# A sparse-attention kernel: the second tile's key products placed behind the first tile's scaling and statistics, and half of the feed-forward weights loaded by another queue

## The chip, the core and the metric

The kernel runs on one core of a Trainium2 chip. A core has TensorE (PE, matrix products), VectorE (DVE), ScalarE (ACT), GpSimd (POOL) and SyncE (SP), which run side by side and wait for each other through semaphores; each takes its own instructions strictly in the order in which they were written into its queue. Sixteen DMA engines move data between the large memory (HBM) and the on-chip memory. The metric is the time of one execution on the device, in microseconds (us); the time before is 1765.6 us, the median of three runs (1764.82 to 1766.44).

## The reference

One layer of attention over a sparse graph, with a feed-forward part. There are 4096 nodes of 512 features, 8 heads of 64. `adj` is a 4096 x 4096 mask with about 17 neighbours per node.

```python
hs, ht = layer_norm(x), layer_norm(h_target)
q = (ht @ Wq + bq) / 8;  k = hs @ Wk + bk;  v = hs @ Wv + bv      # split in 8 heads
logits = where(adj != 0, q . k, -1e30)                            # per head
ctx = softmax(logits) @ v
ht = ht + ctx @ Wo + bo
ht = layer_norm(ht)
out = layer_norm(x + ht + gelu(ht @ W1) @ W2)                     # W1: 512 x 2048, W2: 2048 x 512
```

## The kernel before

The kernel never forms the 4096 x 4096 logits. It works in two stages that overlap a little.

In the first stage (to about 270 us of the trace) PE projects all of `x` to keys and values and ScalarE writes them to a table `kvd` in HBM, one row of 1024 numbers (key and value) per node. Meanwhile the adjacency rows are turned into lists of neighbours, and the nodes are sorted by their number of neighbours. Nodes are then taken in 32 tiles of 128, `TILES`; a tile has a cap, the largest number of neighbours its nodes may have. The first tiles have caps 11, 13, 14, and so on. The tiles are taken in groups (`GROUPS`): the first three tiles alone, the rest mostly in pairs.

The second stage, `attention()`, takes each tile's neighbours in steps of `S = 3`. For each step:

- POOL issues one gather per neighbour (`issue`, L987): 128 rows of `kvd`, 512 KB, into a slot of a ring of 17 slots of on-chip memory. It does so ahead of use, and waits when the slot isn't free.
- VectorE multiplies the gathered keys by the tile's queries (L1277, the *key product*) and sums per head (L1283).
- ScalarE takes the exponential (L1289, L1304 for a tile's first step, and L1255).
- The values are multiplied by these weights: two of three by VectorE (L1224, the *value product*), the third by ScalarE in eight scalings, one per head (L1258).
- PE adds up the values of all neighbours, transposed, in the accumulator `cps` (L1237).

When a tile's last step is done, `finish` divides by the sum of the weights. VectorE takes the reciprocal (L1123); ScalarE spreads it over the features (L1126); PE transposes it (L1132); ScalarE copies it (L1134); VectorE multiplies the accumulator by it (L1137, the *scaling*). PE then multiplies by `wo` (L1149), ScalarE copies the result to `h` (L1155), VectorE takes mean and variance of it (L697, L698) and adds a small constant (L680, in `shifted`); these are the *statistics*. POOL raises to the power -1/2 (L687), VectorE forms the shift factor (L692), ScalarE normalizes (L1169), PE transposes (L1178), ScalarE copies (L1182).

With that, the feed-forward part of the group (`feed`) can start: PE multiplies by `W1` (L1396), ScalarE applies the gelu (L1399, with a load of its function table whenever the function changes), PE multiplies by `W2` (L1405). `end` adds, normalizes and scatters the rows to the output. `front` makes the queries of a later tile: a gather of `h_target`, a normalization by ScalarE (L1026), transposes (L1030, L1033), a product with `wq` on PE (L1040) and a bias on VectorE (L1045).

`W1` and `W2` are loaded in four quarters of 1 MB each (`load_quarter`, L586 and L587). The first two quarters are loaded in the first stage by SP. The last two fit only when the first stage's buffers are free; ScalarE issues them (`weights`), behind the last of the value scalings traced by then (`newest`). They follow each other within the trace at 304 to 306 us.

The order of instructions: the streams (`attention`, `feed`, `weights`, lists for the second half of the nodes) are generators, and `_weave` takes them in turn by the costs that they yield. What comes out is a preferred order. A scheduler then places each instruction on its engine by that order and by a model of when its inputs are ready, so that an instruction may be placed ahead of others traced earlier. `tc.issue_after(ins)`, and the helper `behind([...])` which takes the last of a list, keep it from that: the instruction is placed behind `ins` on the same engine. That is an order only, not a wait for a semaphore.

In the kernel before, `closing` holds the first tile's reciprocal and its scaling. The second tile's next key product is placed behind the reciprocal (`closing[:1]`), the sum that follows behind the scaling, and `closing` is then empty.

Of the kernel before, what the change touches and what calls it, by code (L numbers as in the profile page):

```python
# [19 lines left out]
EPS = 1e-5  # L20
# [423 lines left out]
def adj_resnorm_kernel(  # L444
# [33 lines left out]
    nc = tc.nc  # L478
# [24 lines left out]
    S = 3  # L503
# [29 lines left out]
    with tc.tile_pool(name="keep", bufs=1) as keep:  # L533
# [17 lines left out]
        with ExitStack() as late:  # L551
# [28 lines left out]

            w1, w2 = [], []

            def load_quarter(pool, q, engine=nc.sync):
                w1.append(pool.tile([P, KC, D], F32, name=f"w1_{q}"))
                w2.append(pool.tile([P, KC, D], F32, name=f"w2_{q}"))
                engine.dma_start(w1[q], W1[:, q * D:(q + 1) * D].rearrange("(c p) n -> p c n", p=P))  # L586
                engine.dma_start(w2[q], W2[q * D:(q + 1) * D, :].rearrange("(c p) n -> p c n", p=P))  # L587

# [84 lines left out]
            def rstd_of(pool, mv, n, name):  # L673

                rs = power(pool, mv, n, name)
                return rs, negmean(pool, mv, rs, n, name)

            def shifted(pool, mv, n, name):
                ve = pool.tile([P, n], F32, name=name + "_ve")
                nc.vector.tensor_scalar_add(ve, mv[:, :, 1], EPS)  # L680
                return ve

            def power(pool, mv, n, name, ve=None):
                if ve is None:
                    ve = shifted(pool, mv, n, name)
                rs = pool.tile([P, n], F32, name=name + "_rs")
                nc.gpsimd.tensor_tensor(rs, ve, mhalf[:, :n], ALU.pow)  # L687
                return rs

            def negmean(pool, mv, rs, n, name):  # L690
                nm = pool.tile([P, n], F32, name=name + "_nm")
                nc.vector.scalar_tensor_tensor(nm, mv[:, :, 0], -1.0, rs, op0=ALU.mult, op1=ALU.mult)  # L692
                return nm

            def stats(pool, src, mv, name):
                st = pool.tile([P, 6], F32, name=name + "_st")
                nc.vector.bn_stats(st, src)  # L697
                nc.vector.bn_aggr(mv, st)  # L698
# [19 lines left out]
            def behind(ins):  # L718
                return tc.issue_after(ins[-1]) if ins else nullcontext()
# [261 lines left out]


            recs, tqs, h2Ts, done, ready, latest, newest = {}, {}, {}, set(), [], [], []
            issues, logits, closing = [], [], []

            def gather(dst, table, idx):
                issues[:] = [nc.gpsimd.indirect_dma_start(  # L987
# [121 lines left out]
            def finish(i, p, cps, group, hs, mv):  # L1109


                rec, tq, cap = recs[i], tqs.pop(i), TILES[i][1]
                slow = 0 if i < QUICK else 1
                first = i == 0

                nc.vector.scalar_tensor_tensor(p[:, :cap, :], rec[:, E0:E0 + cap].unsqueeze(2)
                                               .to_broadcast([P, cap, H]), 0.0, p[:, :cap, :],
                                               op0=ALU.is_gt, op1=ALU.mult)
                nc.vector.tensor_reduce(sums[:, i, :], p[:, :cap, :].rearrange("p j h -> p h j"),
                                        AX.X, ALU.add)  # L1120
                ri = sp.tile([P, H], F32, name="ri")
                nc.vector.tensor_scalar_max(ri, sums[:, i, :], SUM_LO)
                recip = nc.vector.reciprocal(ri, ri)  # L1123
                rx = sp.tile([P, KC, P], F32, name="rb", bufs=1)
                rxf = rx.rearrange("p c t -> p (c t)")
                nc.scalar.copy(rxf.rearrange("p (h d) -> p h d", h=H),  # L1126
                               ri.unsqueeze(2).to_broadcast([P, H, HD]))
                for _ in range(0 if first else 1 + slow):
                    yield
                prx = ps.tile([P, KC, P], F32, name="t", bufs=2)  # L1130
                for c in range(KC):
                    nc.tensor.transpose(prx[:, c, :], rxf[:, c * P:(c + 1) * P], ident)  # L1132
                ct = sp.tile([P, KC, P], F32, name="rb", bufs=1)
                nc.scalar.copy(ct, prx)  # L1134
                for _ in range(0 if first else 1 + slow):
                    yield
                scaled = nc.vector.tensor_mul(ct, cps, ct)  # L1137
                if first:
                    closing[:] = [recip.ins, scaled.ins]
                for _ in range(0 if first else 1 + 3 * slow):  # L1140
                    yield
                pa = ps.tile([P, D], F32, name="t", bufs=2)

                for c in range(KC):
                    nc.tensor.matmul(pa[:, c * P:(c + 1) * P], tq[:, D + c * P:D + (c + 1) * P],
                                     ident, is_transpose=True, start=c == 0, stop=False,
                                     skip_group_check=True)
                for c in range(KC):
                    nc.tensor.matmul(pa, ct[:, c, :], wo[:, c, :], start=False,  # L1149
                                     stop=c == KC - 1, skip_group_check=True)  # L1150
                turned.add(i)
                if i > 2:
                    yield
                h = sp.tile([P, D], F32, name="h")
                nc.scalar.copy(h, pa)  # L1155
                yield
                stats(sp, h, mv[:, len(hs), :], "n2")
                hs.append(h)
                if len(hs) < len(group):
                    return  # L1160
                nh = len(hs)
                ve = shifted(sp, mv[:, :nh, :], nh, "n2")
                if i > 2:
                    yield
                rs = power(sp, mv[:, :nh, :], nh, "n2", ve)
                yield
                nm = negmean(sp, mv[:, :nh, :], rs, nh, "n2")
                for j, h in enumerate(hs):
                    nc.scalar.activation(h, h, AF.Identity, bias=nm[:, j:j + 1], scale=rs[:, j:j + 1])  # L1169
                for _ in range(0 if first else 1 + slow):  # L1170
                    yield
                w = len(hs) * P
                h2T = sp.tile([P, KC, 2 * P], F32, name="h2T")
                for k2 in range(KC // 2):
                    pt = ps.tile([P, 2, 2 * P], F32, name="t", bufs=2)
                    for k in range(2):
                        for j, h in enumerate(hs):
                            nc.tensor.transpose(pt[:, k, j * P:(j + 1) * P],  # L1178
                                                h[:, (k2 * 2 + k) * P:(k2 * 2 + k + 1) * P], ident)
                    for k in range(2):  # L1180
                        kc = k2 * 2 + k
                        nc.scalar.activation(h2T[:, kc, :w], pt[:, k, :w], AF.Identity,  # L1182
                                             bias=b2c[:, kc:kc + 1], scale=s2c[:, kc:kc + 1])
                h2Ts[GROUPS.index(group)] = h2T
# [22 lines left out]
            def attention():  # L1207
# [55 lines left out]
                for group in GROUPS:  # L1263
                    hs = []
                    mv = sp.tile([P, 2, 2], F32, name="mv2")
# [3 lines left out]
                    for i in group:  # L1269
                        cps = ps.tile([P, KC, P], F32, name="cps", bufs=2)  # L1270
                        while k < len(SG) and SG[k][0] == i:
                            _, j0, n = SG[k]
                            while i not in tqs:
                                step(fronts, i)
                            kv, tq = kvs.pop(k), tqs[i]
                            with behind(closing[:1]):
                                nc.vector.tensor_tensor(kv[:, :n, :D], kv[:, :n, :D],  # L1277
                                                        tq[:, :D].unsqueeze(1)
                                                        .to_broadcast([P, n, D]), ALU.mult)
                            lg = sp.tile([P, S, H], F32, name="lg")  # L1280
                            latest[:] = [lg[:, 0, 0:1]]
                            with behind(closing):
                                logits[:] = [nc.vector.tensor_reduce(  # L1283
                                    lg[:, :n, :],
                                    kv[:, :n, :D].rearrange("p j (h d) -> p j h d", h=H),
                                    AX.X, ALU.add).ins]
                            closing.clear()
                            if j0 > 0:
                                nc.scalar.activation(p[:, j0:j0 + n, :], lg[:, :n, :], AF.Exp)  # L1289
                            add_up()  # L1290
# [16 lines left out]
                            last = j0 + n == TILES[i][1]  # L1307
# [196 lines left out]
            def fill():  # L1504
# [4 lines left out]
                for cost in _take(ed, FILL * steps):  # L1509
                    yield cost  # L1510

            att = attention()
            _weave((projections(), 0), (prepare(), 0), (fill(), 0))
            src.close()
# [5 lines left out]
            def weights():  # L1520


                for q, pool in enumerate(pools):
                    yield 26.0 if q == 0 else 6.0
                    with tc.issue_after(newest[-1]):
                        load_quarter(pool, q + 2, nc.scalar)

            def other_lists():
                for _ in range(2):
# [44 lines left out]
```

## Time and profile before

| | |
|---|---|
| median of three runs | 1765.6 us |
| the profiled execution | 1769.85 us |
| its span, first to last instruction | 1768.1 us |
| PE busy | 1655.2 us, 94% |
| VectorE busy | 1424.7 us, 81% |
| ScalarE busy | 1234.9 us, 70% |
| GpSimd busy | 1029.6 us, 58% |
| bytes moved by DMA | 461 MB, 260 GB/s over the span |
| mean granted PE clock | 0.975 |

The profiled execution is one execution; its time is that of the span and a little around it. Busy time is the time in which an engine executes something; PE's matmuls overlap, so a busy PE need not be at its peak. PEld is PE's loading of the stationary operand. A wait "X <- Y" means that the instruction X stood idle until Y released it. "issue" is idle time in which the profile shows no wait for another engine. In lists of instructions a form such as `kv<-kv,tq` names what is written and what is read; L1277 is line 1277 of the kernel.

### The profile page before, as it was taken

To read this page: it belongs to the slowest core of one execution; us is meant where nothing else is said; L and a number is where in the kernel's file an instruction comes from. 1 tells how busy PE (TensorE), PEld (TensorE's weight loads), DVE (VectorE), ACT (ScalarE), POOL (GpSimd) and SP (SyncE) were. 2 spreads that over 40 slices of the span, in tenths; PEclk is the share of its full clock that TensorE was granted. 3 is DMA by queue.
4 is the path that set the end of the run, shared out by engine and by line. 5 is a ranking of instruction groups with operands and counts; after the bars stand their busy time and mean duration, and the time that the engine had idled before them with its cause. 6 is when DMAs were issued, how large, how long until landed. Compare 5 with 4: busy or idle time off the path is not lost. (4 is left out here: it accounts for less than half of the span.)

```text
span 1768.1 us, 22715 instructions
## 1 busy us (share of the span) xinstructions
PE 1655.2 (94%) x6978; PEld 1078.4 (61%) x6978; DVE 1424.7 (81%) x2452; ACT 1234.9 (70%) x3133; POOL 1029.6 (58%) x824
## 2 busy tenths in 40 slices
PE   7999996599899999898899999999999999999997
PEld 3444443477676667665566667666666666666665
DVE  6887787489898989897888999989898788999300
ACT  5776663479787988675667878787778687878311
POOL 1000155557565676677787788777787868675101
PEclk9999998799999999998999999999999999999999
DMA  9999978958887897677787888886877767775000
GB/s 352 372 399 361 358 242 288 354 174 285 308 273 275 328 332 266 224 256 239 245 304 270 297 286 313 278 280 222 263 261 249 250 226 260 228 257 201 22 2 26
DMA packets 141610, 461.00 MB, mean 261 GB/s; under 512 B 18036, under 2 KB 23048, under 8 KB 141480
## 3 DMA queue, kind: packets, MB, share of 16 engines
q0 software_dynamic: 96272, 342.33, 57.1%
q1 hardware_dynamic: 37392, 94.06, 15.0%
q10 hardware_dynamic: 7816, 23.08, 3.3%
q8 instruction: 57, 0.93, 0.2%
q14 instruction: 73, 0.60, 0.1%
HBM read 430.61 MB, written 28.79 MB: 260 GB/s over the span
## 5 line engine op out<-in xcount | busy, mean ns | idle before, releaser
L987 POOL DMA_INDIRECT kv<-kvd,rec x603 | 791.8, 1313 | 322.2 <-issue 133.1
L1396 PE MATMUL pf<-h2T,w 128*128 128x256 f32 (+1 forms) x2304 | 467.9, 357 | 4.4 <-ACT h2T L1182 4.0
L1405 PE MATMUL po<-w,gt 128*128 128x512 f32 x1024 | 465.2, 597 | 5.0 <-ACT gt L1399 5.0
L1396 PEld LDWEIGHTS pf<-h2T,w 128*128 128x128 f32 x2304 | 393.8, 191 | 65.8 <-issue 19.5
L1277 DVE TENSOR_TENSOR kv<-kv,tq 128x1536 f32<-128x1536 f32 (+2 forms) x211 | 351.6, 1678 | 65.9 <-DMA kv<-kvd,rec 50.3
L1258 ACT ACTIVATE kv<-kv,pa 128x64 f32<-128x64 f32 x1520 | 391.8, 340 | 3.8
L1283 DVE TENSOR_REDUCE lg<-kv 128x24 f32<-128x1536 f32 (+2 forms) x211 | 350.5, 1669 | 0.2
L1405 PEld LDWEIGHTS po<-w,gt 128*128 128x128 f32 x1024 | 189.3, 192 | 203.2 <-issue 194.7
L1237 PE MATMUL cps<-ident,kv 128*128 128x128 f32 x1828 | 243.2, 279 | 53.9 <-DVE kv L1224 32.5
L1237 PEld LDWEIGHTS cps<-ident,kv 128*128 128x128 f32 x1828 | 217.7, 144 | 121.6 <-issue 48.5
L1224 DVE TENSOR_TENSOR kv<-kv,p 128x1024 f32<-128x1024 f32 (+1 forms) x211 | 251.5, 1196 | 19.7 <-ACT p L1289 19.2
L687 POOL TENSOR_TENSOR n_rs<-n_ve,mhalf 128x2 f32<-128x2 f32 (+2 forms) x53 | 57.6, 1086 | 326.2 <-DVE n_ve L680 143.6
L735 ACT ACTIVATE kv<-kv 128x1024 uint8<-128x1024 int32 x128 | 134.6, 1054 | 54.2 <-DMA kv<-in_adj_dram 22.4
L1399 ACT ACT_TABLE_LOAD x108 | 138.6, 1283 | 1.9
L1399 ACT ACTIVATE gt<-pf 128x512 f32<-128x512 f32 x128 | 76.5, 598 | 82.9 <-PE pf L1396 71.6
L949 PE MATMUL pq<-wk,h2T 128*128 128x512 f32 x256 | 122.6, 622 | 2.8 <-ACT kv L951 1.9
L1149 PE MATMUL t<-wo,rb 128*128 128x512 f32 x256 | 118.3, 606 | 4.9 <-DVE rb L1137 4.9
L949 PE MATMUL pq<-wv,h2T 128*128 128x512 f32 x256 | 115.7, 595 | 5.5 <-DVE rbc L662 2.9
L1040 PE MATMUL t<-wq,tq 128*128 128x512 f32 x256 | 115.2, 593 | 3.4 <-ACT kv L1258 2.2
L744 DVE MAX8 cand<-kv 128x8 uint16<-128x171 uint16 (+1 forms) x384 | 108.9, 327 | 6.3 <-remote 4.1
L1289 ACT ACTIVATE p<-lg 128x24 f32<-128x24 f32 (+2 forms) x179 | 39.3, 219 | 92.2 <-DVE lg L1283 89.2
L949 PEld LDWEIGHTS pq<-wv,h2T 128*128 128x128 f32 x256 | 48.1, 190 | 69.2 <-issue 58.6
(164 smaller groups left out, 1597.1 us busy)
## 6 DMA issues: line engine op xcount, KB each, us to landing
kv<-in_adj_dram SPq DMA_DIRECT2D x128, 512.0 KB
kvd<-tq ACTq DMA_DIRECT2D x23, 512.0 KB
kv<-kvd,rec POOLq DMA_INDIRECT x603
kv<-in_L_gnn_h_target_dram SPq DMA_DIRECT2D x32, 256.0 KB
kv<-in_x_dram SPq DMA_DIRECT2D x15, 512.0 KB
kvd<-kv ACTq DMA_DIRECT2D x9, 512.0 KB
w<-in_L_gnn_W_dram SPq DMA_DIRECT2D x4, 1024.0 KB
w<-in_L_gnn_W_dram ACTq DMA_DIRECT2D x4, 1024.0 KB
```

The source lines that it names most:

```text
L735: nc.scalar.activation(sg, a, AF.Sign, accum_out=dpart[:, i, h:h + 1])
L949: nc.tensor.matmul(pkv, hT[:, kc, j * P:(j + 1) * P], w[:, kc, :], start=kc == 0, stop=kc == KC - 1)
L987: issues[:] = [nc.gpsimd.indirect_dma_start(out=dst, out_offset=None, in_=table[:, :], in_offset=bass.IndirectOffsetOnAxis(ap=idx, axis=0) ...
L1149: nc.tensor.matmul(pa, ct[:, c, :], wo[:, c, :], start=False, stop=c == KC - 1, skip_group_check=True)
L1224: nc.vector.tensor_tensor(v4, v4, p[:, j0:j0 + m, :].unsqueeze(3) .to_broadcast([P, m, H, HD]), ALU.mult)
L1237: nc.tensor.matmul(cps[:, c, :], kv[:, j, D + c * P:D + (c + 1) * P], ident, is_transpose=True, start=j0 + j == 0 and c == 0, stop=j0 + n ...
L1258: newest[:] = [nc.scalar.mul(v, v, pa[:, hd:hd + 1]).ins]
L1277: nc.vector.tensor_tensor(kv[:, :n, :D], kv[:, :n, :D], tq[:, :D].unsqueeze(1) .to_broadcast([P, n, D]), ALU.mult)
L1283: logits[:] = [nc.vector.tensor_reduce(lg[:, :n, :], kv[:, :n, :D].rearrange("p j (h d) -> p j h d", h=H), AX.X, ALU.add).ins]
L1396: nc.tensor.matmul(pf[:, k, :], w1[(f0 + k) // KC][:, kc, (f0 + k) % KC * P:((f0 + k) % KC + 1) * P], h2T[:, kc, :w], start=kc == 0, stop= ...
L1399: nc.scalar.activation(gt, pf, AF.Gelu_apprx_tanh)
L1405: nc.tensor.matmul(po[j], gt[:, k, j * P:(j + 1) * P], w2[(f0 + k) // KC][:, (f0 + k) % KC, :], start=False, stop=f0 + k == FC - 1, skip_g ...
```

## The change

- `load_quarter` takes a list `last`. If it isn't empty, VectorE writes a zero into one column of each of the two weight tiles, placed behind the last of the list; the load of the tile then waits for that write.
- `weights` loads the third and fourth quarter on SP with `last=mark`, where `mark` holds the first tile's scaling. It yields other costs (34 and 2 instead of 26 and 6).
- `shifted` keeps its instruction (the addition of the small constant, L680) in `summed`. When the first tile has come that far, `closing` holds its scaling and this addition.
- The second tile's key products of its first two steps are placed behind the first item of `closing`, those of later steps behind its second. Only the sum of the second step is placed behind the last item. `closing` is not emptied during the second tile.

What this makes of the order on each engine, in the built program: on VectorE the reciprocal is followed by one key product, one value product, the scaling with two of the memsets, one sum, the other two memsets, a value product, the statistics of the first tile, and only then by the key products of the second tile's third, fourth and fifth steps. On PE 23 of the second tile's transposes (L1237) stand behind the first feed-forward matmuls instead of ahead of them. On ScalarE the four weight loads are gone, and exponentials, scalings and gelus of the second and third tile alternate more often. On POOL the power of the first tile stands ahead of nine gathers of which it stood behind. On SP the four weight loads stand between a write of list data and the next adjacency loads. Beyond the third tile the order is unchanged on every engine.

```diff
-            def load_quarter(pool, q, engine=nc.sync):
+            def load_quarter(pool, q, engine=nc.sync, last=()):
                 w1.append(pool.tile([P, KC, D], F32, name=f"w1_{q}"))
                 w2.append(pool.tile([P, KC, D], F32, name=f"w2_{q}"))
+                for w in (w1[q], w2[q]) if last else ():
+                    with tc.issue_after(last[-1]):
+                        nc.vector.memset(w[:, 0, 0:1], 0.0)
                 engine.dma_start(w1[q], W1[:, q * D:(q + 1) * D].rearrange("(c p) n -> p c n", p=P))
                 engine.dma_start(w2[q], W2[q * D:(q + 1) * D, :].rearrange("(c p) n -> p c n", p=P))
...
+            summed = []
+
             def shifted(pool, mv, n, name):
                 ve = pool.tile([P, n], F32, name=name + "_ve")
-                nc.vector.tensor_scalar_add(ve, mv[:, :, 1], EPS)
+                summed[:] = [nc.vector.tensor_scalar_add(ve, mv[:, :, 1], EPS).ins]
                 return ve
...
-            issues, logits, closing = [], [], []
+            issues, logits, closing, mark = [], [], [], []
...
                 scaled = nc.vector.tensor_mul(ct, cps, ct)
                 if first:
                     closing[:] = [recip.ins, scaled.ins]
+                    mark.append(scaled.ins)
...
                 ve = shifted(sp, mv[:, :nh, :], nh, "n2")
+                if first:
+                    closing[:] = [scaled.ins, summed[-1]]
                 if i > 2:
                     yield
...
-                            with behind(closing[:1]):
+                            with behind(closing[:1 if j0 < 2 * S else 2]):
                                 nc.vector.tensor_tensor(kv[:, :n, :D], kv[:, :n, :D],
                                                         tq[:, :D].unsqueeze(1)
                                                         .to_broadcast([P, n, D]), ALU.mult)
...
-                            with behind(closing):
+                            with behind(closing if j0 == S else []):
                                 logits[:] = [nc.vector.tensor_reduce(
...
-                            closing.clear()
+                            if i != 1:
+                                closing.clear()
...
                 for q, pool in enumerate(pools):
-                    yield 26.0 if q == 0 else 6.0
-                    with tc.issue_after(newest[-1]):
-                        load_quarter(pool, q + 2, nc.scalar)
+                    yield 34.0 if q == 0 else 2.0
+                    load_quarter(pool, q + 2, nc.sync, mark)
```

## The prediction

> **What bounds the kernel now.** I read the page's busy shares first, then busy time by stretch, then who waited for whom, then the order of events around the first tile.
>
> ```profile
> PE 1655.2 (94%) x6978; PEld 1078.4 (61%) x6978; DVE 1424.7 (81%) x2452; ACT 1234.9 (70%) x3133; POOL 1029.6 (58%) x824
> ```
>
> TensorE leads, but a share is an average. By stretch (columns: stretch, length, busy us of PE, PEld, DVE, ACT, POOL, then granted clock, DMA share, GB/s):
>
> ```profile
> 305.00:310.00 5.00, 1.53 (x12) 1.30 (x12) 4.10 (x7) 0.92 (x4) 4.07 (x4) 1.00 0.93 323
> 310.00:315.00 5.00, 1.97 (x8) 1.57 (x8) 1.76 (x1) 3.13 (x12) 3.79 (x4) 0.54 1.02 399
> 315.00:320.00 5.00, 0.00 (x0) 0.00 (x0) 1.76 (x1) 0.22 (x1) 2.35 (x3) 0.50 1.03 402
> 320.00:325.00 5.00, 0.00 (x0) 0.00 (x0) 1.12 (x1) 0.00 (x0) 0.00 (x0) 0.50 1.04 402
> 325.00:330.00 5.00, 3.17 (x9) 2.23 (x10) 5.00 (x6) 0.32 (x2) 1.48 (x2) 0.50 1.03 399
> 330.00:335.00 5.00, 5.00 (x24) 3.03 (x22) 5.00 (x7) 4.18 (x15) 2.41 (x4) 0.91 0.95 366
> 600.00:700.00 100.00, 100.00 (x479) 71.25 (x478) 93.26 (x164) 86.35 (x227) 66.82 (x53) 1.00 0.82 293
> ```
>
> Between 310 and 327 every compute engine is nearly idle and DMA alone is full; from 341 on PE is nearly always busy. The waits of 300 to 345 us (total us, times, longest), then PE's waits after 345:
>
> ```profile
> PE cps L1237 <- DVE kv L1224: 17.9, 5, 12.4
> DVE kv L1277 <- DMA kv<-kvd,rec: 11.2, 3, 5.6
> ACT rb L1126 <- issue: 5.9, 1, 5.9
> ```
>
> ```profile
> PE cps L1237 <- DVE kv L1228: 20.8, 4, 8.2
> PE cps L1237 <- DVE kv L1224: 5.7, 1, 5.7
> ```
>
> The second list is short: all PE waits after 345 that it names add to about 45 us of 1423. So a microsecond saved before PE's feed-forward work starts is a microsecond at the end, if the engines keep their distances. Why is it late? VectorE's, then ScalarE's, then PE's order of time (start, length):
>
> ```profile
> 308.97 0.20 DVE L1123 RECIPROCAL ri<-ri 128x8 f32<-128x8 f32 x1
> 310.42 1.76 DVE L1277 TENSOR_TENSOR kv<-kv,tq 128x1536 f32<-128x1536 f32 x1 [1.25 <-DMA kv<-kvd,rec]
> 317.81 1.76 DVE L1277 TENSOR_TENSOR kv<-kv,tq 128x1536 f32<-128x1536 f32 x1 [5.64 <-DMA kv<-kvd,rec]
> 323.88 1.76 DVE L1277 TENSOR_TENSOR kv<-kv,tq 128x1536 f32<-128x1536 f32 x1 [4.30 <-DMA kv<-kvd,rec]
> 325.55 1.22 DVE L1224 TENSOR_TENSOR kv<-kv,p 128x1024 f32<-128x1024 f32 x1
> 326.69 0.69 DVE L1277 TENSOR_TENSOR kv<-kv,tq 128x512 f32<-128x512 f32 x1
> 327.29 0.69 DVE L1137 TENSOR_TENSOR rb<-cps,rb 128x512 f32<-128x512 f32 x1
> ```
>
> ```profile
> 305.62 6.17 ACTq L587 DMA_DIRECT2D w<-in_L_gnn_W_dram  x1
> 311.84 0.62 ACT L1126 COPY rb<-ri 128x512 f32<-128x512 f32 x1 [5.92 <-issue]
> ```
>
> ```profile
> 341.38 0.71 PE L1396 MATMUL pf<-h2T,w 128*128 128x128 f32 x4
> ```
>
> The first tile's scaling (L1137) stands behind key products of the second tile that wait for gathers. These share the DMA engines with 4 MB of weights issued at 304 to 306, and the last issue holds ScalarE for 6 us.
>
> **What the skill says.** The Trainium skill, DMA: Bandwidth & Descriptors (Issuing engines are not separate DMA queues): transfers from ScalarE, SyncE and GpSimd run on the same 16 engines and interleave; another issuer saves only sequencer time. The trace agrees: share 1.02 to 1.04 at about 400 GB/s while both kinds run. So moving the weights to SP speeds no transfer; holding them back does. TensorE: Matmul & The Clock Gate (What's actually happening): the clock halves when idle and returns after some 3.4 us of activity; here 0.50 until PE had been busy from 326.8 to about 330. Perfetto Trace Analysis (Identifying the Most-Contended Engine): matmul busy share overstates how near a kernel is to its limit, weight loading is better. It is 71% in 600:700, so I rest the case on the few waits.
>
> **The change part by part.**
>
> 1. *Weights off ScalarE's queue, behind the scaling.* Four 1 MB loads leave ScalarE and go to SP, after four one-column memsets that follow L1137. SP issues nothing between 275 and 392.6, so nothing stands behind them; adjacency loads are next. Memset: 59 ns (L632), four are 0.24 us; two fit before the next reduction, all while VectorE would wait for h, so nothing; uncovered, 0.24 us. At 400 GB/s 4.2 MB take 10.5 us, so issued at 313 they land by about 325, or 335 when shared evenly with gathers. The third quarter is first read near 342 (below). I cost it at nothing; without that cover, it is the lateness beyond 342.
>
> 2. *Scaling early.* In the new VectorE order only one key product and one value product stand between the reciprocal and L1137. ScalarE: exponentials and two value scalings, then L1126 at 309.5 (0.62), transposes (1.1 at half clock), L1134 after three more scalings (0.6): the factor is there at about 312. VectorE: the key product starts between 309.2 (reciprocal done) and 310.4 (as before, if weights don't delay it), plus 1.7 and 1.15. L1137 starts between 312.1 and 313.3; I take 312.5, because its gathers went out by 303.8 and the previous group's took at most 6 us. Before: 327.3. Gain 14.8.
>
> 3. *Statistics early.* Before, L1137 to the first feed-forward matmul took 341.4 - 327.3 = 14.1: 4.9 matmul L1149, 0.6 copy, then statistics behind a value product and a reduction, and the power on POOL waiting for a gather issue. Now the statistics stand directly behind the copy: 312.5 + 0.7 scaling, + 0.3, + 4.9, + 0.6 = 319.0; statistics 0.9 = 319.9; POOL's power stands ahead of the third tile's gathers, 0.6; VectorE's next key product (1.75) covers it, shift factor at 321.75; then 1.9 as before from L1169 to L1396 = 323.7. That is 11.2 instead of 14.1. Feed-forward starts 17.7 earlier.
>
> 4. *What is moved behind it.* 23 transposes of the second tile (L1237) now follow feed-forward matmuls: 12 took 1.3 to 1.5 us at full clock, so 2.7 us of PE work go back onto the path. ScalarE loads two more activation tables, 7 instead of 5 among the moved instructions, at 1.28: 2.6 us. Following PE through the new order, it reaches the second 12 transposes at about 341 and ScalarE's eight scalings for them end near 337.5, so the loads are hidden with 3 us to spare. A cold clock at 323 could cost up to 1.7 us; the previous idle gap is only about 2 us, less than the 3.5 or so after which the clock fell at 310, so 0.5.
>
> 5. *Second tile's key products late.* They run at 320 to 329 instead of 318 to 327, but their data are there and they are back to back. The second tile's sums end at 336.8 instead of 340.8, and the third tile's query (L1045, before 352.7 because of PE) comes at 337. POOL's first gathers of that tile wait for the power until 320.4; before, three left at 314.5 to 318. The third group's last one waits for ring slot 12, free after PE's first 12 transposes, near 333. It lands by 340 and is wanted near 346: hidden, 6 us to spare.
>
> Sum: 17.7 - 2.7 - 0.5 = 14.5 us (ends 11 and 18: key product late and clock cold, or gathers early and clock warm). Beyond the third tile the order of all engines is as before. The profiled execution took 1769.9 (span 1768.1, 1.8 around it), 4.3 above the median 1765.6; I take the gain off both: span 1753.6, median **1751.1**.
>
> **Rivals.**
> - *The stall moves to ScalarE or PE.* If scalings for the second tile come after 341, PE stops in the middle of feed-forward, as the table loads and exponentials are now strung between them. For: those loads; ScalarE is 4.95 of 5 busy at 365 to 375 before. Against: 3 us of slack. If everything there is 10 us later than I reckon, 7 is lost: 1758.
> - *It is given back.* Adjacency loads and gathers, 0.85 of DMA in 400:600, could pace the kernel, so the early start ends in more waiting. For: that share, and PE at 94.7 of 100 in 400:500. Against: those transfers are released by the engines' own progress, and move with them. 1765.
> - *Slower: POOL's gathers.* The power blocks POOL until the statistics are done, and ring slots now come free behind 64 feed-forward matmuls. If the third tile's third group lands 21 us later than reckoned, past 361, the gain is gone; each us more is lost. Six more: 1772. For: page rows show POOL waiting 143.6 us for such statistics. Against: it needs a landing time of 26 us, against some 6 seen.
>
> **How the numbers follow.** Forecast 0.73 (1747 to 1755), stall moved 0.15, given back 0.05, slower 0.07. A difference under 0.2% (3.5 us) can't be told from none. Faster is 0.73 + 0.15 = 0.88. The range holds the first case and most of the second: 1746.5 to 1759.5.
>
> **What would show it.** L1137 near 312.5, the first L1396 near 324, SP's weight issues at 313; DMA waits of L1277 gone or under 2 us; PE above 4.5 of 5 from 325. Wrong if key products still wait for gathers over 5 us, if PE waits for ScalarE's scalings or for w at 340, or if PE's waits after 345 grow by the same 14 us.

## The result, and the profile after

The changed kernel takes 1755.3 us (median of 14 runs), the kernel before beside it 1766.5 us (14 runs): a ratio of 0.9934, with a 95% interval of 0.9918 to 0.9951. By this ratio it is 11.7 us less, between 8.7 and 14.5 (the two medians differ by 11.2). The forecast was 1751.1 us and 14.5 us less, which is the upper end of that interval.

The profiled execution took 1754.4 us (span 1752.6). Its busy shares say nothing of the gain; TensorE did the same matmuls in a shorter span:

```profile
PE 1651.9 (94%) x6978; PEld 1078.3 (62%) x6978; DVE 1425.2 (81%) x2456; ACT 1236.1 (71%) x3135; POOL 1020.6 (58%) x824
```

The stretches of the changed kernel (columns as in the prediction: stretch, length, busy us of PE, PEld, DVE, ACT, POOL, granted clock, DMA share, GB/s):

```profile
305.00:310.00 5.00, 2.83 (x13) 2.03 (x12) 4.93 (x7) 3.10 (x11) 3.78 (x5) 0.50 0.91 302
310.00:315.00 5.00, 5.00 (x14) 2.95 (x15) 3.56 (x9) 2.37 (x9) 1.64 (x2) 0.76 0.95 349
315.00:320.00 5.00, 2.33 (x19) 1.92 (x17) 3.44 (x6) 1.98 (x6) 2.60 (x2) 1.00 1.03 373
320.00:325.00 5.00, 4.24 (x36) 4.00 (x37) 5.00 (x4) 4.25 (x14) 4.08 (x4) 1.00 1.05 393
325.00:330.00 5.00, 5.00 (x48) 5.00 (x47) 2.08 (x4) 4.92 (x11) 4.08 (x4) 1.00 1.04 402
```

The hole of 310 to 327 is gone. PE works through 310 to 315, and from 321 on it is full; DMA is as full as before (1.03 to 1.05), but no engine waits more than 0.3 us for it between 300 and 345. The waits of 300 to 345 us in the changed kernel (total us, times, longest), of which these are among the longest, hold no DMA wait of the key product (L1285, before L1277):

```profile
DVE kv L1232 <- ACT p L1298: 5.4, 3, 2.8
POOL n_rs L692 <- DVE n_ve L685: 5.3, 1, 5.3
ACT p L1298 <- DVE lg L1291: 4.6, 2, 2.6
```

PE's waits after that are about what they were: all groups together make 46.7 us, against 44.8 before, so at most a small part of the gain is paid back in them. Two of the longest (the same columns, from 330 us to the end):

```profile
PE cps L1245 <- DVE kv L1236: 24.8, 4, 8.4
PE cps L1245 <- DVE kv L1232: 5.6, 1, 5.6
```

VectorE's order of time in the changed kernel (start, length):

```profile
306.78 0.20 DVE L1128 RECIPROCAL ri<-ri 128x8 f32<-128x8 f32 x1
306.90 1.75 DVE L1285 TENSOR_TENSOR kv<-kv,tq 128x1536 f32<-128x1536 f32 x1
308.57 1.22 DVE L1232 TENSOR_TENSOR kv<-kv,p 128x1024 f32<-128x1024 f32 x1
309.70 0.68 DVE L1142 TENSOR_TENSOR rb<-cps,rb 128x512 f32<-128x512 f32 x1
...
316.02 0.69 DVE L702 BATCH_NORM_STATS2 n_st<-h 128x6 f32<-128x512 f32 x1 [2.44 <-ACT h L1161]
...
317.08 1.76 DVE L1285 TENSOR_TENSOR kv<-kv,tq 128x1536 f32<-128x1536 f32 x1
319.31 0.16 DVE L697 SCALAR_TENSOR_TENSOR n_nm<-mv,n_rs 128x1 f32<-128x1 f32 x1 [0.47 <-POOL n_rs L692]
```

The scaling (L1142) stands 2.9 us behind the reciprocal instead of 18.3. SP's queue, where the weights now are, and the first feed-forward matmul on PE:

```profile
310.49 0.38 SPq L589 DMA_DIRECT2D w<-in_L_gnn_W_dram  x1
...
312.69 3.51 SPq L590 DMA_DIRECT2D w<-in_L_gnn_W_dram  x1
```

```profile
321.42 0.71 PE L1405 MATMUL pf<-h2T,w 128*128 128x128 f32 x4 [0.33 <-ACT h2T L1190]
```

One caution on how to compare: in this execution the reciprocal came at 306.8, in the profile of before at 309.0. The change of VectorE's order begins behind the reciprocal; ahead of it the kernels differ only in that the kernel before has issued the weights by then (from 304 us on). From the first tile's first gather to its reciprocal 30.3 us pass in both. In the five profiles of the two the reciprocal came anywhere from 306.8 to 310.2, whichever kernel it was. So I measure all distances from the reciprocal.

### The profile page after: what moved, and what is told of

Its sections match the earlier page's. It is cut to its first block, busy times and chain, and to the rows that moved or that the text cites. A ratio compares the mean times of both kernels' runs of the same rounds, so it can differ in the third digit from the quotient of the medians.

```text
span 1752.6 us, 22726 instructions
## 1 busy us (share of the span) xinstructions
PE 1651.9 (94%) x6978; PEld 1078.3 (62%) x6978; DVE 1425.2 (81%) x2456; ACT 1236.1 (71%) x3135; POOL 1020.6 (58%) x824
## 5 line engine op out<-in xcount | busy, mean ns | idle before, releaser
L1285 DVE TENSOR_TENSOR kv<-kv,tq 128x1536 f32<-128x1536 f32 (+2 forms) x211 | 351.8, 1678 | 54.9 <-DMA kv<-kvd,rec 39.6
L1245 PE MATMUL cps<-ident,kv 128*128 128x128 f32 x1828 | 244.3, 280 | 45.0 <-DVE kv L1236 24.8
L692 POOL TENSOR_TENSOR n_rs<-n_ve,mhalf 128x2 f32<-128x2 f32 (+2 forms) x53 | 53.8, 1014 | 328.6 <-DVE n_ve L685 155.0
L740 ACT ACTIVATE kv<-kv 128x1024 uint8<-128x1024 int32 x128 | 134.4, 1053 | 61.0 <-DMA kv<-in_adj_dram 22.1
L1298 ACT ACTIVATE p<-lg 128x24 f32<-128x24 f32 (+2 forms) x179 | 39.0, 218 | 82.2 <-DVE lg L1291 79.3
```

Source lines behind the costliest of these rows:

```text
L740: nc.scalar.activation(sg, a, AF.Sign, accum_out=dpart[:, i, h:h + 1])
L1245: nc.tensor.matmul(cps[:, c, :], kv[:, j, D + c * P:D + (c + 1) * P], ident, is_transpose=True, start=j0 + j == 0 and c == 0, stop=j0 + n ...
L1285: nc.vector.tensor_tensor(kv[:, :n, :D], kv[:, :n, :D], tq[:, :D].unsqueeze(1) .to_broadcast([P, n, D]), ALU.mult)
```

## The experiments

Three distances in each profile carry the account: from the first tile's reciprocal to its scaling on VectorE; to the first feed-forward matmul on PE; and to the point where PE transposes the second tile's reciprocal (L1132, L1137 in the changed kernel). By then PE has done the work that was moved, so this third distance holds the net effect of the transition. Further profiles of the kernel before and of the changed one are in the table with the experiments. The last column gives ratios to the kernel before, run beside each of them, with 95% intervals.

| kernel | to scaling | to feed-forward | to second tile's transposes | ratio |
|---|---|---|---|---|
| before, two profiles | 18.3, 18.3 | 32.4, 32.6 | 55.0, 55.1 | - |
| changed, first | 2.9 | 14.6 | 39.7 | 0.9934 (0.9918 to 0.9951) |
| changed, second | 2.9 | 14.4 | 41.0 | 0.9909 (0.9884 to 0.9933) |
| changed, third | 2.9 | 14.7 | 39.7 | 0.9924 (0.9902 to 0.9947) |
| order alone | 4.1 | 22.1 | 49.2 | 0.9944 (0.9925 to 0.9963) |
| weights alone, first | 2.9 | 18.7 | 43.4 | 0.9935 (0.9917 to 0.9954) |
| weights alone, second | 2.9 | 19.3 | 44.8 | 0.9937 (0.9911 to 0.9963) |
| weights alone, third | 2.9 | 19.2 | 45.3 | 0.9953 (0.9932 to 0.9974) |
| weights not held | 2.9 | 15.8 | 43.4 | 0.9958 (0.9942 to 0.9974) |
| weights not loaded | 2.9 | 14.6 | 39.7 | 0.9921 (0.9903 to 0.9939) |
| behind the shift factor | 2.9 | 13.6 | 38.7 | 0.9922 (0.9894 to 0.9950) |
| held, on ScalarE | 2.9 | 18.1 | 45.3 | 0.9951 (0.9929 to 0.9973) |

My theory was the prediction's: an instruction that waits at the head of VectorE's queue blocks the ready ones behind it, so the order is what counts, and the weights count only as far as they delay gathers. One rival was that the transfers are the whole matter; another, that ScalarE's queue, held by its issues, is. The edits below are against the changed kernel.

### The order alone

The changed kernel's rules of placement, with the weights on ScalarE as before:

```diff
-                    yield 34.0 if q == 0 else 2.0
-                    load_quarter(pool, q + 2, nc.sync, mark)
+                    yield 26.0 if q == 0 else 6.0
+                    with tc.issue_after(newest[-1]):
+                        load_quarter(pool, q + 2, nc.scalar)
```

> The new order on VectorE alone; the four weight loads stay on ScalarE's queue where they were before, so 4 MB still move beside the gathers and the last issue still holds ScalarE for some 6 us. Theory (the order is what matters: one engine's queue blocked by an instruction that waits): the key product ahead of the scaling waits to about 310.4 as before, L1126's successor on ScalarE runs near 311.8, the scaling starts near 314.6 instead of 327.3 and the first feed-forward matmul comes at 325 to 327; about 1756 to 1760 against 1766, that is 7 to 10 us of the 11.7 gained. Rival (the transfers are what matters: weights and gathers share the DMA engines): no more than 3 us gained, 1763 to 1767, with DMA waits of the key product as long as before. Third view (ScalarE's held queue is what matters): the scaling comes past 317.

It took 1757.9 us, ratio 0.9944. The scaling came 4.1 us after the reciprocal: the order alone takes away all but 1.1 us of its delay, though 4 MB still move beside the gathers and ScalarE is held for 4.3 us. So neither the transfers nor the held queue is the whole matter. The transfers do have a part in the old order: of the 18.3 us before, 11.2 are waits of key products for their gathers, in both profiles. How much of that would be left in the old order with the weights out of the way is open; no run has that pair. But feed-forward began 22.1 us after the reciprocal, at 330.6 and not at 325 to 327. VectorE and GpSimd of this kernel show why (start, length):

```profile
320.79 0.15 DVE L685 TENSOR_SCALAR n_ve<-mv 128x1 f32<-128x1 f32 x1
320.90 1.76 DVE L1285 TENSOR_TENSOR kv<-kv,tq 128x1536 f32<-128x1536 f32 x1
328.19 0.16 DVE L697 SCALAR_TENSOR_TENSOR n_nm<-mv,n_rs 128x1 f32<-128x1 f32 x1 [5.53 <-POOL n_rs L692]
```

```profile
321.92 1.55 POOL L992 DMA_INDIRECT kv<-kvd,rec  x1 [0.97 <-DMA kv<-kvd,rec]
324.01 0.58 POOL L1006 DMA_DIRECT2D rec<-rec  x1 [0.53 <-DMA kv<-kvd,rec]
326.58 0.96 POOL L992 DMA_INDIRECT kv<-kvd,rec  x1 [2.00 <-DMA kv<-kvd,rec]
327.56 0.60 POOL L692 TENSOR_TENSOR n_rs<-n_ve,mhalf 128x1 f32<-128x1 f32 x1
```

The constant was added at 320.8, but the power (L692) stands on GpSimd behind further gathers, and these wait for transfers. The rules fix VectorE's order only; where the power stands among the gathers is the scheduler's choice, and with other costs and another queue for the weights it chose worse. This order with the power ahead of the gathers was not tried, and of the order alone there is one profile only.

### The weights alone

The reverse: the weights on SP behind the scaling, and the rules of placement of before.

```diff
-                if first:
-                    closing[:] = [scaled.ins, summed[-1]]
...
-                            with behind(closing[:1 if j0 < 2 * S else 2]):
+                            with behind(closing[:1]):
...
-                            with behind(closing if j0 == S else []):
+                            with behind(closing):
...
-                            if i != 1:
-                                closing.clear()
+                            closing.clear()
```

> The weights alone: SP loads them behind the first tile's scaling, and the rules for placing the key products are those of before. The scheduler then puts the scaling early by itself (it finds the factor ready sooner), but the second tile's key, value products and sums stand between the first tile's matmul and its statistics. Theory (order matters, and the statistics are a part of their own): scaling near 310 as in the changed kernel, shift factor some 5 us later, first feed-forward matmul at 325 to 327 instead of 321.4; about 1757 to 1760, 2 to 5 us behind the changed kernel. Rival (taking the weights off the gathers' way is all there is): first feed-forward matmul within 1 us of the changed kernel's and the same time, 1754 to 1756.

It took 1754.7 us (ratio 0.9935), less than my theory expected and just the rival's figure. The profile did not look like the rival, though. Feed-forward began 18.7 us after the reciprocal, 4.1 later than in the changed kernel, because sums and products of the second tile stand between the statistics and ahead of the shift factor (L697), which comes 3.1 us later (VectorE of this kernel; where the dots are, a value product and a sum):

```profile
315.69 0.69 DVE L702 BATCH_NORM_STATS2 n_st<-h 128x6 f32<-128x512 f32 x1 [0.33 <-ACT h L1161]
316.30 1.74 DVE L1289 TENSOR_REDUCE lg<-kv 128x24 f32<-128x1536 f32 x1
317.95 0.17 DVE L703 BATCH_NORM_AGGREGATE mv<-n_st 128x2 f32<-128x6 f32 x1
318.04 1.73 DVE L1283 TENSOR_TENSOR kv<-kv,tq 128x1536 f32<-128x1536 f32 x1
319.69 0.15 DVE L685 TENSOR_SCALAR n_ve<-mv 128x1 f32<-128x1 f32 x1
...
322.55 0.15 DVE L697 SCALAR_TENSOR_TENSOR n_nm<-mv,n_rs 128x1 f32<-128x1 f32 x1
```

The two medians were not taken side by side, so I ran this kernel and the changed one beside each other, twice:

> The changed kernel a second time, beside the weights alone and the kernel before on one chip. First feed-forward matmul 14.5 to 15 us after the first tile's reciprocal, as in the first profile. If the 4 us by which its feed-forward starts ahead of the weights-alone kernel reach the end, its median is 3 to 4 us below that kernel's; if the later stages take them back, within 1.5 us.

> The weights alone a second time. Theory one (the placement rules add nothing at the end): median within 1.5 us of the changed kernel run beside it, though its feed-forward work starts 4 us later. Theory two (its first six runs were lucky): 3 to 4 us above the changed kernel.

> The changed kernel a third time, beside the weights alone. If the 4 us lead of its feed-forward work reaches the end, its median is 3 to 6 us below that of the weights alone, as in the second pair (1757.8 against 1763.8); if the second pair was chance, within 1.5 us, as the first medians were (1755.3 and 1754.7, from different calls).

> The weights alone a third time: first feed-forward matmul 18.5 to 19.5 us after the reciprocal, as twice before; its median 3 to 6 us above that of the changed kernel beside it if the statistics' place is worth something at the end, within 1.5 us if not.

The medians were 1757.8 and 1763.8 us the first time, 1763.3 and 1768.4 the second (the kernel before took 1772.5 and 1775.3 there: other chips). So the statistics' place is worth 5 to 6 us at the end in both direct comparisons; the first pair, 1755.3 and 1754.7, did not show it, and its ratios, 0.9934 and 0.9935, don't either. The table's third distance agrees with the direct ones: 39.7 to 41.0 us against 43.4 to 45.3.

The scaling itself is early in this kernel without any new rule: the scheduler moved it once the loads stood elsewhere. So this run does not show what the transfers alone do, as the order changed with them. Each half of the change thus repairs the scaling's delay by itself, and their gains don't add: 9.9 us (order) and 8.3 to 11.5 (weights), against 11.7 to 16.1 for both.

### The weights not held

```diff
-                    load_quarter(pool, q + 2, nc.sync, mark)
+                    load_quarter(pool, q + 2, nc.sync)
```

> As the changed kernel, but the weights are not held: SP issues them as soon as their places are free, between about 272 and 290, where the first tile's gathers move. Theory (DMA was 0.91 to 1.00 busy from 285 on, so 4.2 MB, 10.5 us at 400 GB/s, push the first tile's gathers back, less what fits into the emptier 275 to 285): the first tile's reciprocal comes 5 to 8 us later, and all behind it; 1759 to 1763. Rival (the hold is worth nothing, since the transfers find idle room): within 2 us of the changed kernel, 1753 to 1757.

It took 1758.7 us, 4.0 more than the kernel without these loads that ran beside it (next section). SP issued the four loads at 267 to 274. VectorE's longest wait of 250 to 310 us in this kernel (total us, times, longest) was that of the first tile's key products for their gathers:

```profile
DVE kv L1285 <- DMA kv<-kvd,rec: 10.7, 2, 9.9
```

In the changed kernel's first profile it is one wait of 4.9 us. From the first tile's first gather to its reciprocal 33.6 us pass here, and 30.1 to 30.5 in every other profile: some 3.3 us from the loads. Behind the reciprocal it lost 1.2 us more up to feed-forward, and a further 2.5 up to the second tile's transposes; the clock was 0.50 in the stretch of the first feed-forward matmuls, and 60 of them took 8.5 us instead of 6.9. The direction was as expected; the reciprocal was expected 5 to 8 us late, which is more than the 3.3.

### The weights not loaded

```diff
-                    load_quarter(pool, q + 2, nc.sync, mark)
+                    w1.append(w1[q])
+                    w2.append(w2[q])
```

> As the changed kernel, but the last two quarters of both feed-forward weights are not loaded: the first two quarters are used in their place, so this part of the output is of other weights, and 4 MB, eight one-column writes at most and four issues are left out. All instructions stand as in the changed kernel. Theory (the loads are hidden where they stand now, third quarter wanted at 339): within 2 us of the changed kernel, 1753.5 to 1757. Rival (the moved transfers now hold up the third tile's gathers or the matmuls that read them): faster than the changed kernel by 4 us or more, below 1751.

1754.7 us, ratio 0.9921: no faster than the changed kernel's 0.9909 to 0.9934. All three distances are the changed kernel's. Where the loads now stand they cost nothing that can be measured, although 4 MB of the transfers are missing here: from 321 to 325 us the DMA share of this kernel is 0.00, and at the same distance from the reciprocal it is 1.04 to 1.06 in the changed one.

### Behind the shift factor

In the changed kernel GpSimd's power took 2.07 us, where 0.6 was reckoned from before (there VectorE stood idle beside it); in all three of its profiles a key product ran on VectorE beside it. The Trainium skill, SBUF — State Buffer (Who interferes with whom), says that a VectorE instruction with two inputs from that memory contends with a GpSimd instruction that reads it. So the key products were moved behind the shift factor:

```diff
-                nc.vector.scalar_tensor_tensor(nm, mv[:, :, 0], -1.0, rs, op0=ALU.mult, op1=ALU.mult)
+                summed[:] = [nc.vector.scalar_tensor_tensor(nm, mv[:, :, 0], -1.0, rs, op0=ALU.mult,
+                                                            op1=ALU.mult).ins]
...
-                if first:
-                    closing[:] = [scaled.ins, summed[-1]]
                 if i > 2:
                     yield
                 rs = power(sp, mv[:, :nh, :], nh, "n2", ve)
...
+                if first:
+                    closing[:] = [scaled.ins, summed[-1]]
```

> As the changed kernel, but the second tile's later key products stand behind the shift factor instead of behind the constant addition, so VectorE does nothing while GpSimd takes the power. Theory (the power took 2.07 us instead of 0.6 because a VectorE operation with two inputs from SBUF ran beside it): power 0.6 us, shift factor about 1.4 us sooner, first feed-forward matmul 13 to 13.4 us after the reciprocal instead of 14.6; at the end a gain of 1.4 us or nothing. Rival (GpSimd is slow there for another reason, such as the gathers it has just issued or the full DMA): power still about 2 us, first feed-forward matmul no sooner.

GpSimd in the changed kernel, and then in this one:

```profile
317.21 2.07 POOL L692 TENSOR_TENSOR n_rs<-n_ve,mhalf 128x1 f32<-128x1 f32 x1 [5.26 <-DVE n_ve L685]
```

```profile
322.07 0.58 POOL L692 TENSOR_TENSOR n_rs<-n_ve,mhalf 128x1 f32<-128x1 f32 x1 [5.73 <-DVE n_ve L685]
```

With VectorE idle beside it the power takes 0.58 us, at a DMA share of 1.03, as high as beside the 2.07 us (1.02). The measurement agrees with the skill's statement. From the addition to the shift factor 0.85 us pass instead of 2.34, and feed-forward starts 13.6 us after the reciprocal instead of 14.4 to 14.7. At the end nothing can be told apart: 1757.4 us here, 1757.8 for the changed kernel beside it.

### Held, but issued by ScalarE

```diff
-                    load_quarter(pool, q + 2, nc.sync, mark)
+                    load_quarter(pool, q + 2, nc.scalar, mark)
```

> As the changed kernel, the weights held behind the scaling, but issued by ScalarE instead of SP. In the written order ScalarE then issues two loads ahead of the copy of h and two behind it, and GpSimd has three more gathers ahead of the power. Theory (SP matters as little as it did to the transfers: the issues last about 5 us from 310.5, while ScalarE waits for the matmul and the shift factor anyway): first feed-forward matmul 15 to 17 us after the reciprocal instead of 14.5, median within 3 us of the changed kernel's. Rival (a busy ScalarE queue is what the change cures): the copy of h and the shift come 3 to 6 us late, first feed-forward matmul 18 us or more after the reciprocal, 3 to 6 us slower than the changed kernel.

Feed-forward started 18.1 us after the reciprocal, as the rival said; the median was 1767.0, against 1763.3 for the changed kernel beside it, with intervals that overlap. But the cause is not the one that the rival named. ScalarE of this kernel:

```profile
316.07 0.59 ACT L1161 COPY h<-t 128x512 f32<-128x512 f32 x1 [4.87 <-issue]
...
320.38 0.81 ACT L1031 ACTIVATE tq<-tq,rec 128x512 f32<-128x512 f32 x1 [3.60 <-issue]
321.23 0.81 ACT L1177 ACTIVATE h<-h,n_nm,n_rs 128x512 f32<-128x512 f32 x1
321.95 0.19 ACT L1263 ACTIVATE pa<-lg 128x8 f32<-128x8 f32 x1
324.61 0.22 ACT L1298 ACTIVATE p<-lg 128x24 f32<-128x24 f32 x1 [2.47 <-DVE lg L1291]
...
325.46 1.48 ACT L1190 ACTIVATE h2T<-t,cols 128x128 f32<-128x128 f32 x4
```

ScalarE stood still for 4.9 and 3.6 us while it issued the loads, but the copy of h came 8.2 us after the reciprocal (8.6 in the changed kernel) and the normalization (L1177) 13.4 (12.8): these stops lay for the most part beside waits that were there anyway. Most of the loss came after: the scheduler now put an exponential of the second tile (L1298), with its scalings, ahead of the copy of h2T (L1190), and that exponential waited 2.5 us for a sum on VectorE. So the queue mattered through the order that it left; whether the issues would cost anything with the order kept was not tried. The Trainium skill, DMA: Bandwidth & Descriptors (Issuing engines are not separate DMA queues), puts the price of an issue at the sequencer's time, usually small beside the transfer itself; here the fourth of four 1 MB loads held its engine for 3.4 to 6.8 us on SP and for 2.8 to 6.2 us on ScalarE, over all profiles, and the other three for under 0.8 us each.

### The kernel before, a second time

> The kernel before a second time, for a second profile of the same work. If its first profile was an ordinary one, the first feed-forward matmul comes 32 to 33 us after the first tile's reciprocal again, and the span is within 4 us of 1765; the time between the first stage's last matmul and the reciprocal shows how much of the 2.2 us by which the changed kernel led ahead of the change is chance.

Its distances are those of the first profile (18.3, 32.6 and 55.1), its span 1764.0. The ratio to itself was 0.9992 (0.9975 to 1.0009), which is the size of what chance does here.

This profile also bears on the rival of ScalarE's held queue. ScalarE's last issue, ScalarE's first step after the reciprocal, and VectorE's scaling:

```profile
305.02 2.77 ACTq L587 DMA_DIRECT2D w<-in_L_gnn_W_dram  x1
308.51 0.62 ACT L1126 COPY rb<-ri 128x512 f32<-128x512 f32 x1 [3.29 <-DVE ri L1123]
326.56 0.68 DVE L1137 TENSOR_TENSOR rb<-cps,rb 128x512 f32<-128x512 f32 x1
```

Here the last issue took 2.77 us instead of 6.17 and was over before the reciprocal (308.27), so ScalarE started on it at once; the factor was ready at 311.2, which is 2.9 us after the reciprocal and not 5.5 as in the first profile. The scaling came 18.3 us after the reciprocal all the same: VectorE stood idle for 11.2 of them, with the scaling ready behind key products that waited. In the kernel before, the held queue thus delayed nothing that counted; the prediction's reading, which named it beside the gathers, rests on the one profile.

## Why the prediction was right

*Reading the bound.* That PE is full from feed-forward on, so that what is saved ahead of it is saved at the end, held within what these runs can tell: the transition's third distance fell by 15.3, 14.0 and 15.3 us (from the mean of before, 55.0), and the three ratios make 11.7, 16.1 and 13.5 us. From the second tile's transposes to the end 1404.2 and 1400.6 us pass in the two profiles of before, and 1406.1, 1406.3 and 1402.0 in those of the changed kernel. So some 2 us may be lost again on the way, but single profiles of one kernel differ by 4 us there, and I don't know by what. The other kernels line up as well: 9.7 to 11.6 and 8.3 to 11.5 for the weights alone, 15.3 and 14.0 without loads, 16.4 and 13.8 behind the shift factor, 9.8 and 8.7 on ScalarE; and for the weights not held 11.6 less the 3.3 lost ahead of the reciprocal, which is 8.3, and 7.4. The order alone is the loosest, 5.9 at the transition and 9.9 (6.5 to 13.2) at the end.

*Step 1, the weights at no cost.* Right. They were issued at 310.5 to 316.2; the one load whose landing the trace gives took 13.2 us, and the third quarter was first read at 339.0 without a wait for it. Without the loads nothing is faster. What the step did not price is what the new place avoids: loads that aren't held cost 3.3 us ahead of the reciprocal and more behind it.

*Step 2, the scaling, 14.8 us.* It came 2.9 us after the reciprocal, where 3.5 was reckoned: the key product did not wait for its gathers at all. 15.4 us, right but for 0.6.

*Step 3, the statistics; 17.7 us up to feed-forward.* 17.8 to 18.1 was measured (14.4 to 14.7 against 32.5). Two errors cancelled, so the exact hit is in part luck: the power took 2.07 us instead of 0.6, which made the shift factor half a microsecond later than its cover, the key product, would have; and step 2 was 0.6 better. What the step got wrong in kind was the cover itself. A key product was reckoned to hide the power, and it is what made it slow.

*Step 4, moved behind it, 2.7 and 0.5 us.* Right. From the first feed-forward matmul to the second tile's transposes PE took 22.6 us before, and 25.1 in the changed kernel's first profile: 2.5 us for the 23 transposes. The clock cost nothing in the first and third profile and 1.6 us in the second: there PE's clock was 0.66 in the stretch of the first feed-forward matmuls, and 60 of them took 8.42 us instead of 6.86.

```profile
325.00:330.00 5.00, 5.00 (x32) 5.00 (x32) 4.90 (x5) 4.65 (x17) 3.78 (x5) 0.66 1.04 397
```

PE had been idle for 3.1 us ahead of it, where about 2 were reckoned. The Trainium skill, TensorE: Matmul & The Clock Gate (What's actually happening), has the clock fall after an idle window of about 3.4 us, whose start is not tied to the kernel. The same gap of 3.1 us lowered the clock with the weights not held, and did not in the other two profiles of the changed kernel, nor without loads; so a gap of this length can go either way here. The slack on ScalarE was 2.4 us (scalings done at 335.3, wanted at 337.7), with 3 reckoned.

*Step 5.* The third tile's query (L1050) started at 334.7, which is 27.9 us after the reciprocal; reckoned were 337, or 28.0.

*The sum and the time.* 14.5 us was forecast, 14.0 to 15.3 measured at the transition and 11.7 to 16.1 at the end. The signs that the prediction named came: in the changed kernel's first profile, where the reciprocal is 2.2 us earlier than before, the scaling starts at 309.7, feed-forward at 321.4 and the loads at 310.5, no key product waits for a gather behind the reciprocal, and PE is busy 5.00 of 5 from 325. The median of 1755.3 is 4.2 above the forecast: 2.8 because the gain of these runs was 11.7 and not 14.5, 0.9 because the kernel before took 1766.5 in them and not 1765.6, and the rest because a ratio of all runs isn't a difference of two medians.

*The rivals.* The stall did not move: from 321.4 us to 386 PE is busy for 64.4 of 64.6 us. It wasn't given back, or by no more than some 2 us: the two groups of waits for values shown above are 24.8 and 5.6 us, against 20.8 and 5.7 before, and all of PE's waits 46.7 against 44.8. The slower case, GpSimd's power and gathers in each other's way, didn't arise in the changed kernel; its mirror image did in the order alone, with the power behind the gathers and VectorE's shift factor 5.5 us late.

## What to carry to other kernels

Look for a stretch in which all compute engines idle while DMA is full, find the ready instruction that stands behind a waiting one, and count what a move of it saves at the first point where the bounding engine has done the moved work too; here that number came through to the end within the noise of 2 to 4 us. Two repairs of the same delay don't add, so try each alone. After a rule for one engine's order, read the order on the others as well: twice here an instruction that the rule did not name (GpSimd's power, ScalarE's exponential) held the path up, for 5.5 and 2.5 us.

## What was not expected of the hardware

A power of 128 numbers on GpSimd took 0.58 to 0.60 us with VectorE idle (the kernel before, the order alone, behind the shift factor). Beside a value product that ended at about 321.0 it ran from 319.9 to 321.4 (1.48 us, the weights alone); beside a key product that ended at 318.8 it ran from 317.2 to 319.3 (2.07, the changed kernel). In both it ended some 0.45 us behind VectorE's instruction, as if it did its work only then.

The last of four 1 MB loads held its issuer for 2.8 to 6.8 us, while the first took 0.4. Even two profiles of the same kernel differ in it, 6.2 and 2.8 us for the kernel before; what sets it was not found.
